# A four-layer graph network on one core: the adjacency's transpose moves from TensorE to transposing transfers on SyncE's queue

## The chip, the cores and the metric

The kernel runs on one core of a Trainium2 chip. Its time is the device time of one execution in microseconds (us), and a kernel's time is the median of its runs. The core has five engines: TensorE (PE in the profile, with its weight loads shown apart as PEld), VectorE (DVE), ScalarE (ACT), GpSimd (POOL) and SyncE (SP). SyncE only issues transfers here. ScalarE and GpSimd issue transfers as well as compute. Each engine runs its own list of instructions strictly in order; between engines there are semaphores.

## The reference, cut to what matters

There are 32 graphs ("batches") of 512 nodes with 128 features, each with a 0/1 adjacency matrix of 512 x 512 with about one entry in 32 set. Four layers follow each other, each of them layernorm, relu, a graph layer and a residual sum:

```
h = relu(layernorm(x)); x = x + L0(h, adj)   # p = h(W1-W2), q = h W2;
                                             # max over neighbours j of relu(p_i + q_j + b)
h = relu(layernorm(x)); x = x + L1(h, adj)   # 4 sublayers: adj and adj^T, l2-normed, aggregate h;
                                             # tanh([src, self, dst] @ wu + bu)
h = relu(layernorm(x)); x = x + L2(h, adj)   # rows of adj divided by their sum, times h W, plus bias
h = relu(layernorm(x)); x = x + L3(h, adj)   # 4 GRU steps on adj^T-aggregated messages
```

So each batch needs the adjacency as it lies in memory (`an`), and its transpose (`at`), and the row sums and column sums of it.

## The kernel before, in words

One batch passes through four functions: `prepare` (layer 0 up to the lists of neighbours), `gathers` (the maximum over neighbours), `layer1` (the four sublayers) and `layer23` (layers 2 and 3). They write no instructions at once. Each call is noted with the buffers it reads and writes, and the scheduler `Flow` issues all noted calls of all 32 batches in one order. That order is written out by hand, so to speak: a long table of encoded due times (`FRONT`, `MIDDLE`, `BACK`) gives every noted call a due time, and on each engine the calls go out sorted by it. About four batches are in work at once, at different stages. All calls go out from one line of `Flow.step`, L1038, so nearly all rows of the profile carry that line and one goes by the names of the tiles instead. When the scheduler expects TensorE to wait more than a microsecond, it puts in idle matmuls, `spin` (L1064), whose results nobody reads; they keep TensorE's granted clock up.

Within `prepare`, for batch b:

- ScalarE's queue has loaded `af`, the adjacency in f32, 128 partitions x 4 x 512. A check on VectorE (`junk`) finds whether each entry is 0 or 1.
- ScalarE converts `af` to bf16 in four pieces, `ab`, and sums the rows on the way (`deg`).
- TensorE transposes the sixteen 128 x 128 blocks of `ab` into PSUM (`pat`, against the bf16 identity `identb`), and ScalarE copies them out to `at` in four pieces, summing the columns on the way (L1498 to L1509).
- TensorE counts neighbours by a matmul on `at` (`pc`), ScalarE writes the counts as `cc`, and sixteen small transfers per batch on SyncE's queue spread `cc` to `ccd`. VectorE and ScalarE compare `ccd` with 1 to 4, giving the one-hot matrices `oh`.
- `pkey`, `top`, `at8` and `idx` pick up to seven more neighbours per node, and the table of q goes to memory (`qtab<-qn`, SyncE's queue).

`gathers` takes those seven by indirect transfers on GpSimd's queue (`G<-qtab,idx`), and the first four neighbours of each half tile by matmuls (`pa<-oh,qhl`, 32 per batch), whose results VectorE folds into `acc` by maximum. Then `acc` is transposed back (`px`) and folded into `gm`, and `x1` is the input of `layer1`, which begins with the aggregations `pg` and ends with the products `pu`. `layer23` ends with the sums `xo`, which are stored.

Buffers come in rings: the n-th user of a tag waits until the user `bufs` places before has been read for the last time. `junk` and `ab` share the tag `ab`, which has one buffer, so `ab` of a batch waits for its `junk`, and `junk` of the next batch waits for the last transpose of this one.

The weights are prepared by TensorE, ScalarE and SyncE in the first tens of microseconds, mixed with the first batches (`FastWeights.first`, `rest`, `last`).

Of the kernel before, what the change touches and what calls it, by code (L numbers as in the profile page):

```python
# [13 lines left out]
F32 = mybir.dt.float32  # L14
# [11 lines left out]
P = 128  # L26
# [3 lines left out]
KSLOT = 4  # L30
# [3 lines left out]
NLEFT = 7  # L34
# [3 lines left out]
PERIOD = 81.6923  # L38
# [3 lines left out]
    346.63,  # L42
    (
        "!!!!nz!)U!6%!6:!,G!;8!7/!8i!;1!M*!U=!<I!jA!}3!t<!x.!xW#,y#/W#<|#?x#@z#a4#eA#r##rd#tZ#r_#"
        "sP#sV#s}#{?#oz#q{#ro#sJ$#A#qu#r{$$3$%#$*@#ru#s##~M$$8$+Q$%T#|l$)/$+;$$T$%)$(N$&S$,b$)]$/"
        "x$2$$6n$)}$*|$,?$.=$+_$,|$*h$,0$-]$7{$.z$1H$,{$-I$9y$0h$9<$0+$-L$5M$8[$61$_!$7>$B}$C5$Gb"
        "$Gu$Ja$Ju$P@#Ap$.6$/F$2K$2^$4#$;E$.=$.D$/M$/T$1D$2m$2e$2v$3M$4:$5I$7%$:u$:{$;%$@k$A>$B+$"
        "CR$JN$D>$ML$UQ%.F$H:$E4$Md$O<$FV$Q^$I]$Qw$LA$Vm$Pa$Y;$T>$_N$Uk$bM$WI$dg$Yt$d{$`^$is$c6$k"
        "J$eB$ra$hH$q/$pB$xL$qt$z`$s=${U$u}$~-$y6%%*${<%(;$|_%(y$~f%-0%%c%7]%(t%4q%*:%6X%/^%8R$4h"
        "$7O$7{$8h$=s$8$$>R$@^$?k$DH$9)$C~$E4$F;$Gn$:&$GL$Jd$H`$LM$C]$Jm$Mr$K($P4$G0$M5$P|$R^$S.$"  # L50
        "R0$U2$W$$Ua$Wn$TX$WD$YO$X/$Z;$U:$X^$[($Y/$^1$V/$^i$cr$`X$gv$XY$hh$i6$h~$k_$g9$pw$r#$q2$u"
        "h$j+$tW$vS$vX$w?$ji$w+$yB$xr${j$u*$z-$|U$|}$}L$xa$~9%#K$~P%/N%1~%2-%2U%2l%9O%:A%?q%>1%?R"
        "%?3%3k%@G$tA$t~$z:%._%]=%[m%H%%E%%Gv%D[%H.%I@%J/%D{%I2%LU%PP%JO%Re%So%SE%Ry%TL%U&%Yc%d,%"
        "[C%`s%b:%bi%db%^q%_[%_s%`-%`~%a:%ai%b#%eC%_-%`D%`[%aQ%bE%fi%g;%h<%l0%kC%lU%mU%nP%o_%p[%p"
        "g%pr%q=%q[%r[%s+%sq%tC%tr%uZ%v-%wE%x^%y`%tZ%u-%vD%v[%vs%w.%wt%x/%xk%y/%yF%zm%|)%}7%~8%~C"
        "%~p%~{&!>&!}&#V&$@&%A&(%&)~&*h&+:&+Q&,m&#n&$)&$W&%*&&k&(T&(l&*9&,0&$o&%X&)&&+}&-1&.,&/%&"
        "05&1*&15&1K&1b&2#&3x&4$&:m&;(&;n&<?&=W&=o&@+&D$&:T&;?&;V&<V&=)&>*&?o&C&&F#&<n&GG&Il&K.&L"
        "(&M!&Mz&QQ&S|&Vy&X+&Yi&Yt&Z!&Z9&[D&`t&]9&a,&b(&a@&]X&cb&ci&d&&d?&c|&eY&en&gl&h9&hb&k0&k~"
        "&iA&pY&pr&q-&qC&qZ&rD&rs&w1&yp&|>&|S&|j&}:(#6&}d($1(#Q(%%(&6(%c(%w(&/(&z(&J(&Q(*[(*t(*S("
        ",$(,8(-/(-W(,b(.2(/.(.o(/,(/>(/I(/h(0_(1Y(2T(3&(3>(3U(4((4?(4V(4n(5<(6;(7J(7I(8h(9Y(5@(8"  # L60
        "E(8L(9S(:@(:q(;Q(<>(=3(=>(=I(=T(=s(?2(=`(?-(@((@V(@n(A)(A@(AW(B*(BA(Bl(D%(E8(E4(FF(GF(Bo"
        "(G](E}(IJ(J7(H-(K((Kq(M`(Mk(Mv(O7(OU(P8(N#(OB(Q7(Qg(R8(RO(Sz(T4(Tc(U5(Ua(V_(Y/(Wm(Z=([/("
        "WY(ZA(Xh([O(]<(]0(^-(_!(`3(`T(``(`k(a-(al(`v(ap(bk(c&(c>(cU(cm(d&(dU(eV(f%(g#(gz(h2(i<(j"
        ".(f)(i1(h{(jB(k/(l.(lk(ma(nd(nz(o.(o9(q,(oX(pn(os(qR"
# [4 lines left out]
        0.80,  # L69
        (  # L70
            "!!!!+,!*0!*t!+L!2~!(^!3@"
# [3 lines left out]
        3.00,  # L75
        (
            "!!!!!A!/a!),!,j!3T!([!1Z!.7!/4!-:!01!1.!3(!2+!.d!2W!*J!,=!7L!:1!;n!!>!:[!:{!:f!;)!:Q!=7!"
            ":q!<6!#>!%n!7f!:?!:r!;?!-g!;+!;P!<&!=&!0^!<<!<r!=H!=r!>&!>&!>=!Bn!?5!BY!Cj!)X!;-!?g!A*!A"
            "]!Fh!<w!As!BI!B|!CI!>e!CB!Ca!D7!Db!DM!DN!Dd!I.!FV!H9!I5!Ap!B@!H}!Hr!Id!JE!Jg!Lj!Bm!J|!J["
            "!LN!M[!M0!N8!DZ!ME!MP!NS!O5!Ox!PJ!OK!OK!Ob!Vv!Pg!V;!V[!Eh!I@!P`!Pv!Pk!RT!SA!TK!Tb!Vj!K?!"  # L80
            "T*!T@!T5!U5!U}!VB!Vt!WZ!Mp!V7!VX!Vd!W4!W}!Y9!Y#!ZV!XB!XB!Xj!YK!Y7!Y7!YV"
# [3 lines left out]
        3.74,  # L85
        (
            "!&6!#m!Y2!`N!bw!b2!`r!cm!!!!a$!a0!c%!dh!*,!am!b&!ax!dA!fA!gN!cE!iu!jD!j#!li!bF!j/!j9!jO!"
            "jo!kZ!m3!k?!rA!s2!sx!u?!jo!rL!rc!rx!sf!tb!v?!uq!}/!}f!}:!~g!sF!}P!}Z!}E!~@#!,##$!%Z##@#$"
            "|"
# [5 lines left out]
            "!!!!!M!!O!)5!)^!)I!)q!*K!*D!*)!*R!*m!+)!*f!,6!-@!,I!-i!,s!.!!0^!1M!2>!32!.!!.9!.O!.e!/3!"  # L95
            "3#!3C!3f!48!4V!1W!2u!38!4-!5C!1c!3Z!4N!4Y!60!1n!3O!4C!4f!7h!4q!1y!6!!6a!5l!6;!7U!7w!;O!8"
            "F!<l!?/!:S!6g!76!8U!9s!7u!96!7!!<4!<s!CY!>#!>a!79!>+!Ed!@N!FD!?n!8c!>g!B<!A[!GQ!By!91!9E"
            "!;7!;J!;_!;s!<*!8}!8z!9$!9,!93!9M!:9!9:!9@!9G!9N!;#!;m!9U!9~!:)!:;!=W!@X!=]!=d!=k!=r!DC!"
            "Gr!I`!P6!Iu!>n!G<!L7!Mx!JG!Ss!V[!Q.!RP!U9!W~!ay!YD!Zg!^R!]0!i(!a>!d&!ba!_x!oE!eI!g#!j&!m"
            "b!ul!r&!o(!pJ!sL!{z!tq!vb!x(!yJ#%?!>M!@5!Am!B<!E?!?w!Et!FN!HM!I!!@M!BB!I=!J!!Ir!Jt!Cb!IC"  # L100
            "!Jm!Kv!KR!M}!LV!MR!Nj!Mk!OU!M8!P<!Ph!PS!R*!J|!LJ!RW!S&!SK!TX!Mf!OO!Sc!UD!U~!VM!QH!V9!W9!"
            "WA!X$!Sw!WY!YG!YT!Z3!Qc!VM!Ym!]<!Z&!^(!X%![o!^=!`(!^Z!`p!^e!_a!bY!_w!cE!_F!`A!d2!a!!dz!^"
            "G!a:!be!ef!co!fR!bV!cr!eu!g>!gz!ne!oq!p.!p9!pD#&,#(N#+0#*/#*n#*N!$Z#+c!L<!K[!Ly!N|!S_!T/"
            "!S,#-^#-r#-7#.*#.P#.W#-V#.I#.q#2Z#.j#3|#5*#5S#4]#44#6-#6u!fL#5i#66#6A#6{#:L#7*#8L#8X#8e#"
            "9.#9G#9`#9y#:<#7E#8r#8~#9:#9S#9l#:)#:5#;S#:B#:N#:Z#:g#:t#;##;0#;<#>]#;I#;U#;b#;n#;{#<+#<"
            "7#<D#>~#<P#=,#<]#=9#?B#?n#@P#@=#@i#AY#A8#AC#B9#BD#B##Be#C!#CL#B[#CD#CQ#Cj#D&#D3#De#G<#Gi"
            "#Bh#C^#Cv#D?#DK#DX#Dq#E.#Ed#C!#D}#E:#EF#ES#El#Ex#F)#H9#E`#F5#FA#FM#FZ#Fg#Fs#G!#GF#G0#G`#"
            "Gl#H<#H{#IJ#J.#I}#JM#K0#K*#K<#Kl#Kw#K[#LN#L9#Mf#LF#M:#MG#NQ#Nk#R1#R=#RJ#Rj#LS#M.#MS#M`#M"
            "l#NE#N^#Nw#P4#La#O&#O3#OL#OX#Or#P.#PG#SD#O@#Oe#O~#P;#PS#P`#Pm#R##RE#Py#S%#Q)#S3#QT#U)#RV"
            "#UT#S_#V##T.#TY#U=#V^#W4#Wt#Wn#X##XZ#Xf#XB#Xs#Y)#YQ#Xz#Y_#Yl#Z?#Zd#[-#[]#[v#_r#YR#Yx#Z(#"  # L110
            "Zp#Z}#[P#[j#]=#bV#_;#_N#_Z#_h#_y#`0#`=#`I#by#`U#`b#`o#`{#a+#a7#aD#aP#cR#a]#es#aj#f;#b9#h"
            ")#be#hT#c4#i##c`#ih#d/#j7#da#jc#eG#g!#gb#k2#kv#lX#lh#n,#n6#nA#vE#wo#w4#wZ#x9#x2#wS#y@#xX"
            "#yR#{?#yY#|L#~)#~R#}3#}[$!,$&N$#u$)n$**$*A$*W$+F$+v$,1$1;$3z$5-$5Z$5q$6+$7V$6i$9|$9+$8t$"
            "9h$:E$:|$:u$;F$:n$;?$;a$>D$;X$?`$?t$@j$A7$@A$An$B[$B:$BE$BP$Cs$DI$E@$F;$G5$Ge$G|$H7$Hf$H"
            "}$I7$IN$Iz$Jq$L$$L!$M3$NU$If$M7$M.$NE$O2$P`$P!$Q}$Rr$R}$S,$S7$SU$T9$SB$U9$W/$W^$Wu$X0$XG"
            "$X_$Y1$YH$Ys$[-$]($]U$^6$_-$Y`$^:$^B$`w$b-$`:$cw$dd$eg$er$e}$g%$gE$h($f,$g1$iU$in$j)$j@$"
            "jW$k@$kW$l6$la$mu$o*$o&$p8$q6$le$p#$q?$r2$rz$s&$sx$tm$ub$ul$uw$v%$vE$w($v1$w7$x2$xI$xa$x"
            "x$y3$yJ$z4$zy${H$|F$~S$}f%!b%#_${K%!N%!V%#]%$I%$B%%:%&%%(,%(<%(R%)$%*~%*I%*d%*/%+H"
# [3 lines left out]
        5.36,  # L122
        (
            "!)C!/!!1K!0]!0H!04!23!2,!1D!2$!2E!2^!2M!3k!5I!4|!4S!4*!<G!@#!A;!BL!C=!9x!:&!:2!:=!N@!DZ!"
            "D`!Df!Dl!O?!BC!BI!CF!D7!ZZ!T8!Ub!V(!Wv!`#!U]!U~!V-!Wp!`l!WD!Vu!bz!de!af!b5!cb!c?!d~!f-!h"
            "$!hx!ja!ba!cF!dg!fe!d*!eG!c4!cx!f(!k1!h%!kn!cK!dM!lN!j#!r+!gE!cc!kn!m/!sH!tU!rh!a_!c&!ga"
            "!lM!lb!n*!q@!FJ!cy!d#!d+!d2!lX!qf!d9!d@!dG!dN!k$!kn!ho!jT!jb!kN!nC!o/!jZ!ji!j{!k%!s1!sz!"
            "uE!wZ!uZ!t@!w=!w[#)m#(G#+3#,U!v-#39!zc#0S!}$#3p!~I#9F#3x#<&#5>#>m#6a#@N#:!#B1#<_#Dy#?I#G"
            "o#A*#I5#Bj#Jt#Et#N/#HK#PV#In#R,#KP#S^#No#W.#Q3#Y=#Re#[`#T:#^=#Wg#`r#[$#d^#_E#gO#`h#i:!mM"
            "!nH!nz!ng!rP!ov!q]!te!rF!ue!m_!oO!tU!wb!tn!xM!pl!rD!v`!zM!w2!{9!y.!z*!|^!~%!~h!yl!~=#!S!"  # L130
            "~`##H!tz!yb#!7#$5##N#$}!{E!~`##f#%i#$C#&U#)w#*s#+H#+4#,4#*X#+c#,|#,5#-i#!|#)A#,d#/+#-6#/"
            "s#+O#,k#0s#1I#1K#25#.I#1c#5r#8d#:C#0h#8|#;/#97#<;#1b#2}#<M#=&#<e#?$#4=#93#<|#?n#BG#D<#FF"
            "#G$#G0#G;#iY#jv#mQ#m2#l_#l?!!!#nO!wn!y/!xN!w1#ml#n<#_!#pD#p1#oy#pr#pd#q=#pk#q5#r,#rW#r$#"
            "tv#v##u.#uV#vM#w&#wo#rZ#vc#vn#vy#w0#w]#wx#yK#yz#zL#z{#{d#{{#|6#}M#xJ#{6#{M#|M#|e#||#}7#}"
            "f#~4#}N#}}#~x$!r$$$$$v$%$$%0$%:$%Y$&<$&J$(7$(N$(f$)8$)f$*g$,!$,Y$&y$(}$)O$)}$*8$*O$*~$+P"
            "$-:$,Q$,i$-{$/1$0?$1?$1J$1U$1a$2!$2p$3!$4}$5O$69$7:$7h$8!$8Q$:Q$3:$3k$58$5g$5~$6P$6h$7P$"
# [8 lines left out]
        ),  # L145
    ),
    (
        22.66,
        (
            "!!!!2O!+u!,-!-z!/-!/H!/A!/O!/V!5t!7Z!/i!8h!FS!;q!97!=C!Q=!Sx!UL!V<!XB!b(!b3!bC!bN!c+!be!"  # L150
            "bq!bv!b|!c]!b>!bY!b`!bk!dL!c$!c1!c<!d+!e9!c+!c6!c|!d%!f%!e>!do!i;!}&!g@!ej!hu!|L#/r#0U#2"
# [2179 lines left out]
```

## Time and profile before

| what | value |
|---|---|
| median of 3 runs | 2818.99 us (2816.03 to 2822.98) |
| the profiled execution | 2812.02 us |
| its span, first to last instruction | 2810.3 us |
| mean granted clock of TensorE | 0.993 |
| TensorE busy | 2730.7 us (97%), 11169 matmul rows |
| VectorE busy | 2450.0 us (87%) |
| GpSimd, ScalarE busy | 1640.5 us (58%), 1284.4 us (46%) |

A table by stage is read so: each row is a stretch of the span, and for each engine it gives the busy microseconds and, in brackets, the number of instructions. A group gives the line, the engine, the operation, the names written and read, the shape, how often it came, then the busy time and the mean duration of one, then the idle time of that engine right before it. TensorE's matmuls overlap, so the duration of one (from its start to its modelled end) is longer than the time until the next one starts; the room that a matmul takes is the distance between starts. SPq and ACTq are the issues of transfers on SyncE's and ScalarE's queues.

### The profile page before, as it was taken

To read this page: it belongs to the slowest core of one execution; us is meant where nothing else is said; L and a number is where in the kernel's file an instruction comes from. 1 tells how busy PE (TensorE), PEld (TensorE's weight loads), DVE (VectorE), ACT (ScalarE), POOL (GpSimd) and SP (SyncE) were. 2 spreads that over 40 slices of the span, in tenths; PEclk is the share of its full clock that TensorE was granted. 3 is DMA by queue.
4 is the path that set the end of the run, shared out by engine and by line. 5 is a ranking of instruction groups with operands and counts; after the bars stand their busy time and mean duration, and the time that the engine had idled before them with its cause. 6 is when DMAs were issued, how large, how long until landed. Compare 5 with 4: busy or idle time off the path is not lost.

```text
span 2810.3 us, 36776 instructions
## 1 busy us (share of the span) xinstructions
PE 2730.7 (97%) x11169; PEld 1743.4 (62%) x11169; DVE 2450.0 (87%) x5739; ACT 1284.4 (46%) x2623; POOL 1640.5 (58%) x1892
## 2 busy tenths in 40 slices
PE   7799999999999999999999999999999999999997
PEld 4466666666666666666666666666665656666675
DVE  7788999999999999999999999999998988988533
ACT  7644444444444444444444444445444344434333
POOL 5676665566656556665656665665666666665311
PEclk9999999999999999999999999999999999999999
DMA  7743334343344443434444333344433433333100
GB/s 170 131 77 74 68 75 88 83 81 79 70 76 89 89 84 78 81 70 77 89 81 92 73 79 70 83 90 80 92 68 73 91 85 80 62 61 57 36 4 9
DMA packets 188177, 217.59 MB, mean 77 GB/s; under 512 B 28826, under 2 KB 136516, under 8 KB 187972
## 3 DMA queue, kind: packets, MB, share of 16 engines
q0 software_dynamic: 47104, 92.34, 24.4%
q1 hardware_dynamic: 73540, 64.62, 7.8%
q10 hardware_dynamic: 67328, 58.20, 6.6%
q8 instruction: 91, 1.49, 0.2%
q14 instruction: 114, 0.93, 0.1%
HBM read 164.32 MB, written 17.17 MB: 65 GB/s over the span
## 4 chain that ended last, share of the span: by engine, by line
PE 82%; DVE 7%; POOL 2%; issue 2%; ACT 2%; DMA 1%; SPq 0%; DVEq 0%; ACTq 0%; POOLq 0%
PE pg L1038 25%; PE pu L1038 19%; PE pk L1038 14%; PE pa L1038 7%; PE phn L1038 4%; PE pxn L1038 3%; PE ph L1038 2%; PE pq L1038 2%; PE pf L1038 1%; PE pt L1038 1%; DVE nn L1038 1%; DVE acc L1038 1%; PE po L1038 1%; PE px L1038 1%; PE pkey L1038 1%
## 5 line engine op out<-in xcount | busy, mean ns | idle before, releaser
L1038 POOL DMA_INDIRECT G<-qtab,idx x744 | 794.5, 1068 | 464.7 <-DVE gm L1038 277.1
L1038 DVE TENSOR_TENSOR acc<-acc,pa 128x512 f32<-128x512 f32 x992 | 676.3, 682 | 57.8 <-PE pa L1038 32.0
L1038 PE MATMUL pa<-oh,qhl 128*128 128x512 f32 x1024 | 490.8, 504 | 5.9 <-DVE oh L1038 2.5
L1038 PE MATMUL pg<-an,hi 128*128 128x512 f32 (+1 forms) x1072 | 471.4, 445 | 1.8 <-ACT hi L1038 1.4
L1038 PE MATMUL pu<-ag,w 128*128 128x512 f32 (+1 forms) x952 | 445.8, 574 | 0.1
L1038 PE MATMUL pg<-an,lo 128*128 128x512 f32 (+1 forms) x1072 | 401.9, 389 | 1.4 <-DVE lo L1038 1.4
L1038 DVE TENSOR_SCALAR oh<-ccd 128x1024 fp32r<-128x1024 bf16 x492 | 338.6, 699 | 15.0 <-DMA ccd<-cc 7.5
L1038 ACT ACTIVATE xn<-x,shift,rstd 128x128 f32<-128x128 f32 x512 | 222.0, 486 | 173.0 <-POOL shift L1038 138.6
L1038 PEld LDWEIGHTS pa<-oh,qhl 128*128 128x128 f32 x1024 | 190.9, 190 | 133.9 <-issue 57.4
L1038 PE MATMUL pg<-at,hi 128*128 128x512 f32 (+1 forms) x672 | 273.5, 422 | 0.4 <-DVE lo L1038 0.3
L1038 PEld LDWEIGHTS pg<-an,hi 128*128 128x128 f32 x1072 | 202.0, 188 | 97.0 <-issue 42.1
L1038 PE MATMUL pk<-mT,g_ih 128*128 128x512 f32 (+1 forms) x528 | 257.4, 584 | 1.2 <-ACT mT L1038 1.2
L1038 ACT ACTIVATE gate<-pk,bsum 128x512 f32<-128x512 f32 (+1 forms) x264 | 176.5, 673 | 175.8 <-PE pk L1038 138.5
L1038 PE MATMUL pk<-h,g_hh 128*128 128x512 f32 (+1 forms) x528 | 253.0, 586 | 0.4 <-ACT h L1038 0.2
L1038 PE MATMUL pg<-at,lo 128*128 128x512 f32 (+1 forms) x672 | 250.0, 387 | 1.1 <-POOL lo L1038 0.7
L1038 PEld LDWEIGHTS pu<-ag,w 128*128 128x128 f32 x952 | 168.8, 190 | 113.1 <-issue 94.5
L1038 PEld LDWEIGHTS pg<-an,lo 128*128 128x128 f32 x1072 | 201.7, 188 | 57.1 <-issue 10.3
L1038 ACT COPY mT<-pg 128x512 f32<-128x512 f32 (+1 forms) x164 | 94.2, 574 | 273.3 <-PE pg L1038 237.5
L1038 DVE TENSOR_TENSOR gm<-gm,G 128x128 f32<-128x128 f32 x744 | 212.8, 292 | 2.0 <-DMA G<-qtab,idx 1.9
L1038 POOL TENSOR_TENSOR rstd<-rstd,mhalf 128x4 f32<-128x4 f32 x128 | 143.7, 1126 | 106.8 <-DVE rstd L1038 62.1
L1038 DVE TENSOR_TENSOR ag<-pg,rbc 128x512 f32<-128x512 f32 (+1 forms) x272 | 173.8, 650 | 22.7 <-PE pg L1038 22.4
L1038 POOL TENSOR_SCALAR zc<-gate 128x512 f32<-128x512 f32 (+1 forms) x132 | 81.0, 614 | 165.1 <-ACT gate L1038 164.5
(179 smaller groups left out, 5245.0 us busy)
## 6 DMA issues: line engine op xcount, KB each, us to landing
ccd<-cc SPq DMA_DIRECT2D x512, 64.0 KB
an<-in_adj_dram POOLq DMA_DIRECT2D x128, 256.0 KB, 4.2
af<-in_adj_dram ACTq DMA_DIRECT2D x31, 1024.0 KB
x<-in_x_dram ACTq DMA_DIRECT2D x64, 256.0 KB
rbc<-scal SPq DMA_DIRECT2D x32, 512.0 KB
G<-qtab,idx POOLq DMA_INDIRECT x744, 3.7
qtab<-qn SPq DMA_DIRECT2D x32, 256.0 KB
out_dram<-xo ACTq DMA_DIRECT2D x32, 256.0 KB
```

The lines of the kernel that those rows point to most:

```text
L1038: op.fn(*(real(v) for v in op.args), **{k: real(v) for k, v in op.kw.items()})
```

## The change

Six things change. The sixteen transposes per batch on TensorE, and their PSUM banks `pat`, are gone. `ab` becomes four tiles of 128 x 512 in a ring of two buffers. Each is transposed by one transposing transfer, issued by SyncE from SBUF to SBUF, into a new tile `abt` (128 x 4 x 512 bf16, one buffer), and ScalarE reads `abt` in place of `pat` when it writes `at`. `junk` moves to the tag of `abt`, and for the first batch to the tag of `oh`. A one-column square root on ScalarE comes first of all, so that its function table is loaded first. The input `x` of the first two batches stays in SBUF instead of being loaded a second time; `qn` moves to the tag `xn0`. And the encoded order of all instructions is new, from a scheduler whose entries for transfers were changed as well. The new constants (`KSLOT`, `NLEFT` as tuples, `KEPT` empty) keep their values, so that what they switch does not change.

```diff
-KSLOT = 4
+KSLOT = (4, 4)
-NLEFT = 7
+NLEFT = (7, 7)
+KEPT = ()
...
     def first(self):
+        F.act.activation(self.own([P, 1], F32, "root"), self.ones[:, 0:1], AF.Sqrt)
...
     def load(b):
-        xt = F.tile(mid, [P, NT, D], F32, tag="xin", name=f"x_{b}")
+        xt = F.tile(mid, [P, NT, D], F32, tag="x1" if b < 2 else "xin", name=f"x_{b}", bufs=2 if b < 2 else 1)
...
-        junk = F.tile(big, [P, NT * N], BF16, tag="ab", name=f"junk_{b}")
+        junk = F.tile(
+            big, [P, NT * N], BF16, tag="oh" if b == 0 else "abt", name=f"junk_{b}", bufs=3 if b == 0 else 1
+        )
...
-        ab = F.tile(big, [P, NT, N], BF16, tag="ab", name=f"ab_{b}")
+        abs_ = []
         for t in range(NT):
+            ab = F.tile(big, [P, N], BF16, tag="ab", name=f"ab_{b}_{t}", bufs=2)
             F.act.activation(
-                ab[:, t, :], af[:, t, :], AF.Identity, accum_out=deg[:, 0, t : t + 1]
+                ab, af[:, t, :].bitcast(F32) if b in KEPT else af[:, t, :], AF.Identity,
+                accum_out=deg[:, 0, t : t + 1],
             )
+            abs_.append(ab)
...
-        for half in range(NT // 2):
-            pt = bank(0, [P, 2, N], BF16, f"pat_{b}_{half}")
-            for u in range(2):
-                jt = 2 * half + u
-                for it in range(NT):
-                    F.tr(
-                        pt[:, u, it * P : (it + 1) * P],
-                        ab[:, it, jt * P : (jt + 1) * P], W.identb,
-                    )
-                F.act.activation(
-                    at[:, jt, :], pt[:, u, :], AF.Identity, accum_out=deg[:, 1, jt : jt + 1]
-                )
+        abt = F.tile(big, [P, NT, N], BF16, tag="abt", name=f"abt_{b}")
+        for it in range(NT):
+            F.sync.dma_start_transpose(out=abt[:, :, it * P : (it + 1) * P], in_=abs_[it])
+        for jt in range(NT):
+            F.act.activation(
+                at[:, jt, :], abt[:, jt, :], AF.Identity, accum_out=deg[:, 1, jt : jt + 1]
+            )
...
-        x1 = F.tile(mid, [P, NT, P], F32, tag="x1", name=f"x1_{b}", bufs=2)
-        F.act.dma_start(out=x1, in_=x[b].rearrange("(t p) d -> p t d", p=P))
+        x1, an = xt, af
+        if b >= 2:
+            x1 = F.tile(mid, [P, NT, P], F32, tag="x1", name=f"x1_{b}", bufs=2)
+            F.act.dma_start(out=x1, in_=x[b].rearrange("(t p) d -> p t d", p=P))
```

## The prediction

> **What bounds the kernel now.** I read the page's busy table first, then the windows by stage, then TensorE's waits in the steady part, then the rows that the change removes, then the start.
>
> The busy table:
>
> ```profile
> PE 2730.7 (97%) x11169; PEld 1743.4 (62%) x11169; DVE 2450.0 (87%) x5739; ACT 1284.4 (46%) x2623; POOL 1640.5 (58%) x1892
> ```
>
> 97% is an average, so the windows come next: the start, the steady part, the run-out and the last batches. Columns are the stretch, its length, busy us of PE, PEld, DVE, ACT and POOL, granted clock, DMA share, GB/s.
>
> ```profile
> 0.00:326.80 326.80, 283.92 (x1291) 184.33 (x1292) 270.52 (x658) 178.39 (x366) 203.15 (x258) 0.96 0.55 107
> 326.80:2091.00 1764.20, 1761.43 (x7081) 1120.42 (x7081) 1629.34 (x3801) 817.93 (x1669) 1080.26 (x1243) 1.00 0.40 80
> 2091.00:2634.00 543.00, 530.27 (x2080) 329.51 (x2078) 478.18 (x1093) 228.02 (x468) 332.39 (x359) 1.00 0.38 73
> 2634.00:2810.30 176.30, 155.12 (x722) 109.09 (x720) 71.99 (x191) 60.05 (x123) 24.66 (x34) 0.97 0.03 9
> ```
>
> In the steady 1764 us TensorE is idle for 2.8 us. VectorE is at 92%, ScalarE at 46%, the DMA engines at 40%. The view of TensorE's own waits from 500 to 1980 us has two rows, 1.5 us in all:
>
> ```profile
> PE ph L1038 <- DVE h L1038: 1.3, 2, 1.0
> PE pk L1038 <- ACT mT L1038: 0.2, 1, 0.2
> ```
>
> So in this part nothing but TensorE's own work sets the pace: 18 batches in these 1480 us, 82.2 us each. Work taken from TensorE there is worth its whole time, until VectorE's 75.6 us per batch (its busy time in the window from 1500 to 1581.7) becomes the bound, 6.6 us lower.
>
> **Part 1: the transposes leave TensorE.** The built program has 512 matmuls `pat` and 512 weight loads less, and 128 transposing transfers on SyncE's queue more, so the change does what it says. The view of tile `pat` gives the duration, the timeline of TensorE from 1509 us the room:
>
> ```profile
> L1038 PE MATMUL pat<-identb,ab x512: 216/219/314, 14.2 to 2533.9; 128*128 128x128 bf16 x171
> ```
> ```profile
> 1510.39 0.39 PE L1038 MATMUL pat<-identb,ab 128*128 128x128 bf16 x4
> 1510.62 0.50 PE L1038 MATMUL pf<-ident,f 128*128 128x128 f32 x3
> 1510.95 0.33 PE L1038 MATMUL pat<-identb,ab 128*128 128x128 bf16 x3
> 1511.12 0.28 PE L1038 MATMUL ph<-ident,h 128*128 128x128 f32 x1
> ```
>
> One lasts 219 ns but four make room for the next kind after 1510.62 - 1510.39 = 0.23 us, three after 0.17: 57 ns each. A batch loses 16 x 57 ns = 0.91 us, all batches 29.2 us. For batches 0 to 3 the transposes stand before TensorE is saturated (about 240 us), so on the path lie 28 x 0.91 = 25.5 us.
>
> The Trainium skill speaks against this: "VectorE: DVE Perf Modes", section "The three transpose paths", gives 390 ns for a bf16 128x128 on TensorE and 1309 ns through the DMA crossbar, and advises TensorE where PSUM will do. By its 390 ns the removal would be worth 16 x 0.39 = 6.2 us a batch, some 175 us in 28; the row above decides against that, because transposes overlap. By its 1309 ns a transfer of four blocks would take an estimated 5.2 us, which no row here shows.
>
> **Part 2: what hides the new transfers.** Each moves 128 KB, four per batch. The trace of before has no transposing transfer, so bounds are from neighbours, here the queues and three issue rows (KB each, us to landing):
>
> ```profile
> q0 software_dynamic: 47104, 92.34, 24.4%
> q1 hardware_dynamic: 73540, 64.62, 7.8%
> an<-in_adj_dram POOLq DMA_DIRECT2D x128, 256.0 KB, 4.2
> G<-qtab,idx POOLq DMA_INDIRECT x744, 3.7
> two<-qtab,idx POOLq DMA_INDIRECT x24, 7.5
> ```
>
> q1, which carries SyncE's kinds of transfers by its bytes, moved 64.62 MB in 7.8% of 2810 us, 219 us: 128 KB take 0.4 us. At q0's rate (92.34 MB in 686 us) they take 1.0 us. So the moving is 0.4 to 1.0 us, the landing 3.7 to 7.5 us. I take 1.0 and 4.2 us, the slower queue and the nearest size above. That is 4 us of DMA engines per batch where 60% of 82 us is free.
>
> The landing is hidden. In the new order `at` of a batch is read some 40 ScalarE instructions after its last `ab`, beginning just after the store of the batch three before. In the trace of before the like stretch, from the first `acc` copy (1540.8) to the next `xo` (1595.5), lasts 55 us; the landing would have to grow tenfold. ScalarE's own work stays: `at` from PSUM took 598 ns each, `ab` from SBUF 620, so 4 x 22 ns more, on an engine busy at 46%.
>
> Not so far from the path is SyncE's queue. In the new order the first transfer of batch b+1 stands ahead of the first `ccd<-cc` of batch b, the second and third stand among its other `ccd` pieces, and the first must also wait for `junk` of b+1 on VectorE, which now shares a buffer with `abt`. Behind it queue 16 `ccd`, `qtab`, `rbc`, `row`; VectorE's `oh` and then TensorE's `pa` wait for `ccd`. The queue in before:
>
> ```profile
> 1529.52 3.67 SPq L1038 DMA_DIRECT2D ccd<-cc  x6
> 1533.23 0.56 SPq L1038 DMA_DIRECT2D scal<-sct  x1
> 1533.89 5.27 SPq L1038 DMA_DIRECT2D ccd<-cc  x4
> ```
>
> A piece takes 0.61 us to issue, four 2.4 us, and at a gather's 3.3 us for 64 KB (`gm`, the nearest row of that size) they land at about 1535.3. The first `oh` starts at 1537.78: 2.5 us of slack. An issue of 0.4 to 1.3 us (an ordinary row, or two of them) fits in; I count nothing.
>
> **Part 3: the start.** The windows from 0 to the first `acc`, then to the moments at which batches 0, 1 and 2 have `x1`:
>
> ```profile
> 0.00:31.40 31.40, 21.91 (x108) 12.35 (x108) 17.07 (x59) 18.04 (x51) 10.61 (x44) 0.95 0.62 181
> 31.40:107.00 75.60, 54.61 (x265) 34.17 (x264) 59.65 (x128) 56.01 (x113) 48.67 (x56) 0.89 0.90 162
> 107.00:172.00 65.00, 56.49 (x339) 45.33 (x339) 55.23 (x135) 33.43 (x62) 39.20 (x46) 1.00 0.50 93
> 172.00:237.00 65.00, 62.46 (x237) 37.81 (x238) 57.30 (x142) 31.35 (x63) 47.12 (x50) 0.95 0.41 72
> ```
>
> Here VectorE leads, 189 us busy of 237, and latencies show.
> - Later: batch 0's chain. In before `ab` began at 13.4 us and the last `at` at 21.7. Now four conversions (0.8 us each) go through two buffers, so the third waits for the first transfer: two round trips of about 4 us, then four `at` of 0.8 us. Sixteen small weight loads (0.25 to 0.45 us each in the first microseconds) stand between the first two transfers on SyncE. Together 8 to 13 us; I take 10.
> - Later: the new order lets TensorE begin batch 0's `pg` only after batch 1's `px`. By counting instructions times the room of each, 74 us of TensorE's work then lie between the `px` of batches 1 and 2, in place of 61, while VectorE has 66. That is up to 8 us.
> - Earlier: most of layer 1's weights are prepared while batch 0 waits, so that VectorE's idle time of 16 us in the second window and 10 in the third can shrink, by some 8. The order has 3.5 us less VectorE work ahead of batch 2's `px` (197 us against 201). The second function table load (1.28 us at 15.34) leaves the chain. Two loads of `x` (256 KB each) fall away in the window with DMA at 0.90, price 0 to 1 us.
> - `junk` of batch 0 in another buffer: it ended at 10.6 us and `ab` began at 13.4, so nothing.
>
> Bounds: if the weights hide all of the later start, -3.5 - 1.3 = -5; if nothing is hidden, 13 + 8 - 5 = +16. I take 10 + 8 - 8 - 3.5 - 1.3, about +5. A sign of a longer start is that the order has 161 idle matmuls there, 94 before; how long the gaps are it does not tell.
>
> **Part 4: the end.** The latest 30 us of TensorE's work, from the last but one batch's result on, are the same in both orders, and the idle matmuls there are 48 in place of 54. I count nothing.
>
> **The sum.** -25.5 + 5 = -20.5 us on the profiled execution's 2812.0 (span 2810.3), so 2791.5. The median of the three runs shown is 2819.0, 7.0 us above the profiled one; carried over, **2798.5 us**.
>
> **Rivals.**
> - *The start eats the gain.* It loses the whole 16 us or some more, say 18: 2819 - 25.5 + 18 = 2811.5, no change. For it: 67 more idle matmuls, and TensorE's late `pg`. Against it: VectorE leads there and has less to do.
> - *SyncE's queue holds `ccd` up (slower).* One mechanism: a transposing transfer keeps SyncE or its rings longer than 2.5 us, so that `oh` comes late and TensorE, which has no slack, waits at `pa` in each of 28 batches. It decides from 2.5 + 20.5/28 = 3.2 us per transfer. At 4.2 us it costs 28 x 1.7 = 48: 2798.5 + 48 = 2846; at 7.5 us 28 x 5 = 140. For it: the place in the queue and that no such transfer is in the trace. Against it: by both queues' rates the moving is 1 us at most.
> - *The start gets shorter:* -25.5 - 5 = -30.5, 2788.
>
> **The numbers.** The main case 0.66, the shorter start 0.08, the start that eats the gain 0.12, SyncE's queue 0.14. From no change this measurement can tell about 0.3%, 8.5 us (2810.5 to 2827.5). Faster 0.74, within 0.12, slower 0.14. The main case alone, with the start's bounds, is 2788 to 2810. The range goes from 2784 (shorter start and 4 us of scatter) to 2824, which takes in the case of no change and leaves out most of SyncE's.
>
> **What would show it.** Right: in the steady part the batches follow at about 81.3 us, TensorE's idle there stays at a few us, `pat` is gone, `at<-abt` waits for no DMA, the third batch's `x1` comes at about 242 us. Wrong: rows "DVE oh <- DMA ccd" or "PE pa <- DVE oh" in each batch; the transposing rows on SPq above 2.5 us; or an idle TensorE in the first 240 us beyond 16 us more than before.

## The result, and the profile after

The changed kernel takes 2829.07 us (median of 6 runs, 2827.85 to 2831.26) against 2818.18 us for the kernel before on the same chip (6 runs): a ratio of 1.0038, 95% interval 1.0025 to 1.0051. It is 0.4% slower, where 0.7% faster was forecast. The profiled execution took 2828.67 us (span 2827.0) against 2812.02 before, 16.7 us more, where the medians are 10.9 apart: before's profiled execution lies 6.2 us under the median of its runs here, after's at its median. Some 6 us of what follows on the two traces are thus scatter between executions.

The same views as before the prediction, now of the kernel after. The busy table and the windows (stretch, length, busy us of PE, PEld, DVE, ACT and POOL, granted clock, DMA share, GB/s):

```profile
PE 2723.7 (96%) x10703; PEld 1719.5 (61%) x10718; DVE 2432.8 (86%) x5739; ACT 1268.1 (45%) x2623; POOL 1730.0 (61%) x1892
```
```profile
0.00:326.80 326.80, 282.16 (x1241) 181.05 (x1251) 263.98 (x633) 177.34 (x364) 196.53 (x246) 0.96 0.62 115
326.80:2091.00 1764.20, 1746.48 (x6684) 1090.83 (x6683) 1606.95 (x3783) 791.44 (x1654) 1158.49 (x1241) 1.00 0.44 86
2091.00:2634.00 543.00, 523.75 (x2015) 328.77 (x2014) 482.41 (x1114) 232.96 (x472) 343.83 (x366) 1.00 0.41 78
```

In the steady stretch TensorE is now idle for 1764.2 - 1746.5 = 17.7 us, where it was 2.8. The view of TensorE's waits from 500 to 1980 us names what it waits for:

```profile
PE ph L1051 <- ACT f L1051: 5.0, 16, 0.3
PE ph L1051 <- DVE h L1051: 3.3, 2, 2.8
PE pf L1051 <- ACT f L1051: 0.7, 2, 0.4
```

A transpose `ph` waits for ScalarE's `f` in 16 of 18 batches; before, it did not once. The new transfers do not occur in this view. Their own view, tile `abt`, shows what they cost and who waited for them:

```profile
L1051 SPq DMA_TRANSPOSE abt<-ab x128: 1189/1216/4964, 13.6 to 2479.5; - x128
L1051 ACT ACTIVATE at<-abt x128: 612/618/643, 33.1 to 2487.4; 128x512 fp32r<-128x512 bf16 x128
...
who waited for it (us, times):
  POOL dm L1051: 22.6, 4
  ACT ab L1051: 8.2, 2
```

SyncE issues one in 1.2 us in the median, inside the 0.4 to 1.3 us of the prediction. VectorE's `oh` waits for a `ccd` transfer once in the whole run, for 3.8 us. Both waits of `ab` for a transfer lie in the first 101 us. So in the steady part nothing was lost at the new transfers themselves; the time went elsewhere.

Two measures tell where. The first is the period, the median distance between the last `xo` rows of successive batches, batches 5 to 20. The forecast was 81.3 us; it is 82.27, where before had 82.20. The second is the time of the last `xo` of a batch against the kernel before: 11.5 us later at batch 0, 16.0 at batch 3, 16.2 at batch 9, 21.5 at batch 11, 20.8 at batch 21, 16.7 at the end. So the start lost 16 us, the steady part gained nothing and lost 5 us once, and batches 22 to 24 gained some 4.

### The profile page after: what moved, and what is told of

The parts are those of the page before. It is cut to its first block, busy times and chain, and to the rows that moved or that the text cites. A ratio compares the mean times of both kernels' runs of the same rounds, so it can differ in the third digit from the quotient of the medians.

```text
span 2827.0 us, 36274 instructions
## 1 busy us (share of the span) xinstructions
PE 2723.7 (96%) x10703; PEld 1719.5 (61%) x10718; DVE 2432.8 (86%) x5739; ACT 1268.1 (45%) x2623; POOL 1730.0 (61%) x1892
## 3 DMA queue, kind: packets, MB, share of 16 engines
q1 hardware_dynamic: 143172, 81.41, 11.7%
## 4 chain that ended last, share of the span: by engine, by line
PE 79%; DVE 10%; POOL 4%; issue 4%; ACT 3%; DMA 1%; SPq 0%; DVEq 0%; ACTq 0%; POOLq 0%
PE pg L1051 24%; PE pu L1051 18%; PE pk L1051 13%; PE pa L1051 6%; PE phn L1051 3%; PE pxn L1051 3%; PE ph L1051 2%; DVE nn L1051 2%; DVE acc L1051 2%; PE pq L1051 2%; PE pf L1051 1%; POOL G L1051 1%; PE pt L1051 1%; PE po L1051 1%; PE pkey L1051 1%
## 5 line engine op out<-in xcount | busy, mean ns | idle before, releaser
L1051 POOL DMA_INDIRECT G<-qtab,idx x744 | 829.3, 1115 | 380.6 <-DVE gm L1051 172.7
L1051 PE MATMUL pa<-oh,qhl 128*128 128x512 f32 x1024 | 482.3, 497 | 15.9 <-issue 6.3
L1051 PE MATMUL pg<-an,hi 128*128 128x512 f32 (+1 forms) x1072 | 464.1, 439 | 4.4 <-ACT hi L1051 3.7
L1051 PE MATMUL pg<-an,lo 128*128 128x512 f32 (+1 forms) x1072 | 413.4, 392 | 0.0
L1051 DVE TENSOR_SCALAR oh<-ccd 128x1024 fp32r<-128x1024 bf16 x492 | 344.8, 703 | 7.1 <-DMA ccd<-cc 3.8
L1051 PE MATMUL pg<-at,lo 128*128 128x512 f32 (+1 forms) x672 | 265.3, 398 | 1.5 <-POOL lo L1051 1.3
L1051 PE MATMUL pk<-h,g_hh 128*128 128x512 f32 (+1 forms) x528 | 245.1, 586 | 0.6 <-ACT h L1051 0.5
L1051 POOL TENSOR_TENSOR rstd<-rstd,mhalf 128x4 f32<-128x4 f32 x128 | 162.4, 1269 | 114.7 <-DVE rstd L1051 89.0
L1051 POOL TENSOR_TENSOR lo<-xn,hi 128x512 fp32r<-128x512 f32 x96 | 123.2, 1283 | 139.4 <-ACT hi L1051 138.6
```

Of the source, the lines that this page charges most:

```text
L1051: op.fn(*(real(v) for v in op.args), **{k: real(v) for k, v in op.kw.items()})
```

## The experiments

Theory A: the new order is at fault; it brings waits of its own that take the freed time, in the start and in each batch. Theory B: the transposing transfers slow something, GpSimd above all, whose semaphores last 208 ns in place of 59 and whose gathers `G` 1135 ns in place of 1058. Theory C: TensorE's time was never worth its whole, since other engines' chains lie right behind it. All kernels were timed against the kernel before on their own chip.

| kernel | ratio to before, 95% interval | median, us | period, us |
|---|---|---|---|
| before | 1 | 2812.7 to 2818.2 by chip | 82.20 |
| after | 1.0038 (1.0025 to 1.0051) | 2829.07 | 82.27 |
| after, again | 1.0041 (1.0029 to 1.0053) | 2831.74 | 82.28 |
| e1: old order, transfers | 0.9940 (0.9926 to 0.9953) | 2796.39 | 81.38 |
| e2: transposes twice | 1.0074 (1.0061 to 1.0088) | 2834.04 | 83.11 |
| e4: after, plain copies | 1.0066 (1.0052 to 1.0080) | 2832.60 | 82.28 |
| e5: after, more TensorE work | 1.0138 (1.0123 to 1.0154) | 2851.78 | 83.33 |
| e7: e1 with more batches | 0.9935 (0.9923 to 0.9947) | 2800.48 | 81.40 |
| e8: after, batch 0 on TensorE | 1.0046 (1.0033 to 1.0059) | 2831.51 | 82.28 |
| e9: e1, table and `x` | 0.9937 (0.9924 to 0.9950) | 2800.70 | 81.40 |
| e12: work in the wait | 1.0063 (1.0047 to 1.0079) | 2830.00 | 82.26 |
| e14: work elsewhere | 1.0077 (1.0061 to 1.0093) | 2835.37 | 82.49 |

Four kernels with the order of after have periods of 82.27 to 82.28: the period is good to about 0.02 us, far better than the total time.

**e1_old_order_dma: the transfers in the old order.** The kernel before, with its table of due times, and only the transposes of batches 5 to 25 moved.

```diff
+        if b in MOVED:                       # range(5, 26)
+            abt = F.tile(big, [P, NT, N], BF16, tag="abt", name=f"abt_{b}")
+            for it in range(NT):
+                F.sync.dma_start_transpose(out=abt[:, :, it * P : (it + 1) * P], in_=abs_[it])
...
+    junk = max(due[s - 10], at + 0.9)
+    ab[2], ab[3] = max(ab[2], ab[0] + 7.0), max(ab[3], ab[1] + 7.0)
+    return (due[: s - 10] + [junk] + ab + due[s - 5 : s] + [t + 0.9 for t in ab] + ...
```

> Kernel before, its start and its order, with the transposes of batches 5 to 25 alone moved to SyncE's transposing transfers (each due 0.9 us after its ab; the four at follow each other at the place of the first; junk writes to the buffer of abt; some small rings are shortened for room). TensorE loses 21 x 0.91 = 19.1 us of work. Theory A (the new order is at fault, not the transfers): about 2799 us (2795 to 2806), batches follow at 81.3 us. Theory B (the transfers themselves slow other engines, GpSimd above all): no gain, 2817 or more, period 82.2 or more, and GpSimd's semaphores and gathers longer as in after. Theory C (other engines' chains lie right behind TensorE, so that its time is worth only a part): 2808 to 2818, period between 81.7 and 82.2, and TensorE idle some tenths of a us in each batch.

Measured: 2796.39 us, 17.4 below before, period 81.38. TensorE's busy time in the steady stretch of e1:

```profile
326.80:2091.00 1764.20, 1758.23 (x6815) 1120.60 (x6815) 1640.51 (x3841) 824.72 (x1677) 1095.33 (x1252) 1.00 0.47 87
```

and its waits from 500 to 1980 us:

```profile
PE ph L1055 <- DVE h L1055: 0.8, 1, 0.8
PE pf L1055 <- ACT f L1055: 0.3, 1, 0.3
PE pk L1055 <- ACT mT L1055: 0.2, 1, 0.2
```

TensorE stays busy, idle 6.0 us in 1764, and the waits at `f` in every batch are not there. This is theory A: the same transfers bring 0.82 us per batch of the 0.91 forecast, if the order stays. It is also faster than both kernels of the case. Order is not all that sets e1 apart from after: after also has other buffers for `qn` and `hi2`, and no run took these apart from the order. The waits that after shows are for `f`, `mT` and `h`, whose tags are the same in both.

**e2_pat_twice: the price of a transpose.**

```diff
                 for it in range(NT):
-                    F.tr(pt[:, u, it * P : (it + 1) * P], ab[:, it, jt * P : (jt + 1) * P], W.identb)
+                    for again in range(1 if b < 4 else 2):
+                        F.tr(pt[:, u, it * P : (it + 1) * P], ab[:, it, jt * P : (jt + 1) * P], W.identb)
```

> Kernel before with each of the transposes of the adjacency done twice in batches 4 to 31 (448 more, same place, same data). If a transpose makes 57 ns of room and TensorE sets the pace (theories A, B, C alike for more work): 448 x 57 ns = 25.5 us more, about 2844 us (2840 to 2848). If one costs what it lasts (219 ns) it is 98 us more, about 2916. If TensorE does not set the pace in before: under 2825.

Measured: 20.3 us more, somewhat under the 25.5 expected. In the steady part the price is exact: the period rises from 82.20 to 83.11, by 0.91 us for 16 transposes: 57 ns each, as read from the distances between starts. Neither the 219 ns that one lasts nor the 390 ns of the Trainium skill ("VectorE: DVE Perf Modes", "The three transpose paths") is what it costs here.

**e4_plain_copy: are the transposing transfers to blame?**

```diff
-            F.sync.dma_start_transpose(out=abt[:, :, it * P : (it + 1) * P], in_=abs_[it])
+            F.sync.dma_start(
+                out=abt[:, :, it * P : (it + 1) * P], in_=abs_[it].rearrange("p (t c) -> p t c", c=P)
+            )
```

> Kernel after, with each transposing transfer replaced by a plain transfer of the same bytes between the same buffers at the same place (leaves out the transposition, so that at holds the matrix untransposed, and the count that would start the slow path is set to 0). Theory A (order) and C: as after, 2829 us (2824 to 2833), period 82.2. Theory B (transposing transfers slow others): about 2805 to 2815, period 81.3 to 81.7, GpSimd's semaphores and gathers as short as in before (59 ns, 1058 ns).

Measured: ratio 1.0066, period 82.28, so no gain at all from taking the transposition away. GpSimd's groups from 500 to 1980 us, first in e4, then in after, are alike:

```profile
L1051 POOL DMA_INDIRECT G<-qtab,idx x432 | 490.0, 1134 | 204.3 <-DVE gm L1051 70.9 <-issue 50.0 <-DVE xo L1051 36.8
```
```profile
L1051 POOL DMA_INDIRECT G<-qtab,idx x432 | 490.1, 1135 | 204.6 <-DVE gm L1051 71.7 <-issue 56.0 <-DVE xo L1051 37.0
```

while e1, with transposing transfers, has 1055 ns and gains. The longer rows do not come from the transposition, and theory B falls. Nor does the order alone make them: e5, below, has the order of after and 1062 ns.

**e5_after_more_pe: has TensorE room in after?**

```diff
+        if 4 <= b < 25:
+            for half in range(2):
+                more = bank(0, [P, 2, N], BF16, f"more_{b}_{half}")
+                for k in range(8):
+                    F.tr(more[:, k // 4, (k % 4) * P : (k % 4 + 1) * P], W.identb, W.identb)
```

> Kernel after with 16 more bf16 transposes of 128 x 128 on TensorE in each of batches 4 to 24 (of the identity, results read by nobody), just ahead of at: 21 x 0.91 = 19.1 us of work put back. If TensorE sets the pace in after: about 2848 us. Theories A and C (TensorE waits for other engines in each batch, so has room): a part of it, 2829 to 2840.

Measured: 1.0138 against 1.0038 to 1.0041 for after, some 27 us more, and the period 1.06 us longer. Those were other chips; against e4, which has the same order and ran on the same chip, it is 19.2 us more, for the 19.1 us of work put in. This went against what theories A and C had been read to say: although TensorE waits in each batch, its work still counts in full. The waits are links of TensorE's own chain, not room beside it. With e1 this settles theory C too: in either order TensorE's work is worth its time.

**e12_work_in_wait and e14_work_elsewhere: the wait itself.** The timeline of after around one of the waits (start, us, engine, line, operation, in brackets the idle time before it):

```profile
1364.72 1.02 PE L1051 MATMUL pu<-ag,w 128*128 128x512 f32 x2
1365.18 1.03 PE L1051 MATMUL pa<-oh,qhl 128*128 128x512 f32 x2
1365.78 0.69 ACT L1051 ACTIVATE f<-pu,bu 128x512 f32<-128x512 f32 x1 [1.66 <-PE pu L1051]
1366.52 0.30 PE L1051 MATMUL ph<-ident,h 128*128 128x128 f32 x1 [0.31 <-ACT f L1051]
```

`pu` ends, ScalarE makes `f` of it, and the order gives TensorE only two `pa` to do meanwhile. `ph` of another batch comes next and starts 0.05 us after `f` has ended; the profile names `f` as what released it. It reads nothing that `f` writes; a PSUM bank that `f` has to read first would make it wait so, which is not shown. By the distances between starts 0.42 us are lost there. The two kernels put four more transposes into this place, and into a place 2 us later.

```diff
                 if s == 0 and t == NT - 1 and int(name.split("_")[1]) in TWICE:      # range(8, 26)
+                    for k in range(4):
+                        F.tr(pt[:, t, :], src[:, t, :], W.ident)
...
+                due = due[:26] + [due[26] - EARLIER] * 4 + due[26:]                   # 2.06 in e12, 0.001 in e14
```

> Kernel after, with one f32 transpose (the fourth pt of layer 0) done five times instead of once in batches 8 to 25, the four extra ones (4 x 0.11 = 0.44 us) right ahead of the ph of the batch four before, where the trace of after shows TensorE waiting 0.42 us for ScalarE's f (16 of 18 batches). If that wait of the new order is real and stands in TensorE's own chain, the work fits into it: 0 to 2 us above after (1.004 to 1.005 of before). If TensorE's waits are not where the time goes (its work counts wherever it stands, as in e5): 18 x 0.44 = 7.9 us more, 1.0068 of before.

> The same four extra transposes in batches 8 to 25 of kernel after, but right ahead of the fourth pt itself, some 2 us of TensorE's work later, where the trace shows no wait. Both theories: 18 x 0.44 = 7.9 us more than after, 1.0068 of before; it is the price against which e12 is held.

Measured: the totals differ by 5.4 us with overlapping intervals (both 1 to 2 thousandths above what was expected), so the periods decide: 82.26 with the work in the wait, the same as after, and 82.49 with it elsewhere. There its rows take 0.44 us (the five `pt` from 1454.38 to the next start at 1454.85, where one had 0.03), of which half is made up by short waits that after has behind this place and e14 has not. The row `ph` after the added work in e12 has no idle time before it:

```profile
1448.20 0.60 PE L1054 MATMUL pt<-ident,xn 128*128 128x128 f32 x4
1448.69 0.30 PE L1054 MATMUL ph<-ident,h 128*128 128x128 f32 x1
```

So the wait is real, it stands in the chain, and its length is what the rows show.

**e8_after_pat0: the start.** Batch 0's transposes alone back on TensorE, its conversions one after the other.

```diff
+            if b == 0:
+                ab = whole[:, t, :]
...
+                at = [15.0, 15.8, 16.6, 17.4]
+                due = due[:20] + [11.1, 11.9, 12.7, 13.4] + due[24:29] + [
+                    v for t in at for v in [t - 0.9] * 4 + [t]
+                ] + due[37:]
```

> Kernel after, with batch 0's transposes alone put back on TensorE and their conversions one after the other, so that batch 0's at is there at about 22 us in place of 36; all else and its order as in after. If the first batch's two round trips of transfers (10 us in the prediction) make the start late: the first acc comes some 10 us earlier and the time falls by up to 10 us (0.9965 of after). If the new order makes it late (it has the weights' work ahead of batch 0's on each engine): less than 2 us, and the first acc stays near 47 us.

Measured: as after (1.0046 against 1.0041 on the same chip). The last `at` of batch 0 starts at 19.5 us in place of 37.1, and still the first `acc` comes at 52.1 us, 48.7 in after on that chip. The round trips of the first batch, 10 us in the prediction, are not what makes the start late.

**e11_after_again: after, once more.**

> Kernel after, unchanged, on the same chip as the others of this call, to compare e8 with: 1.0038 of before (1.0025 to 1.0051).

Measured: 1.0041, as the first time.

**e7_old_order_more and e9_old_order_root_x: what else in the old order?** e7 moves the transposes of batches 5 to 31, e9 adds the square root's table and the kept `x` to e1.

```diff
-MOVED = range(5, 26)
+MOVED = range(5, 32)                                                                   # e7
...
+        F.act.activation(self.own([P, 1], F32, "root"), self.ones[:, 0:1], AF.Sqrt)    # e9
...
+        x1 = xt
+        if b >= 2:
```

> As e1_old_order_dma, but with the transposes of batches 5 to 31 moved (27 in place of 21), the conversions of a batch further apart (10 us in place of 7 between the first and the third). Theory A (in the old order a freed us of TensorE is worth what e1 showed, 17.4 us for 21 batches, 0.83 each): the last batch has nothing behind it and batches 26 to 30 have other, tighter orders, so up to 5 x 0.83 = 4 us less than e1's 2796.4 at its before of 2813.8, that is 0.9925 of before. If the conversions' waits for the two buffers stall ScalarE in the last batches: as e1 or up to 8 us more.

> As e1_old_order_dma, with two more parts of the change in the old order: the square root's table first on ScalarE, and x of batches 0 and 1 kept in place of a second load. By the prediction -1.3 us for the table and 0 to -1 for the loads: 1.3 to 2.3 us below e1. If the table load does not lie on the path or what is saved is waited for elsewhere: as e1.

Measured: 0.9935 and 0.9937 against e1's 0.9940, all within each other's intervals. The six more batches bring nothing that can be told, and neither do the table and the loads, priced at 1.3 to 2.3 us. What is left to make the start of after some 16 us later is its order, with the transfers of batches 1 to 4 and the new buffers, which no run took apart from it.

## Why the prediction was wrong

**Part 1, the price: right.** 57 ns a transpose is what e2 shows, and e1 gives back 0.82 of 0.91 us per batch.

**Part 1, the sum: the step that failed.** "Work taken from TensorE there is worth its whole time" was read from a trace in the old order, and the 25.5 us were then booked for a kernel with a new one. The new order has waits that no row of before could show. In a batch of after, 0.42 us are lost at `ph <- f`, 0.28 at `pk <- mT` (a row with 12 to 26 ns of idle time, but started 0.28 us late), and 0.25 in a stretch of four `pu` and three `ph` between two `pa`, 0.95 us together; in e1 the first two are seen once each at most. The 0.91 us that the transposes left were gone again, and the period stayed at 82.27. The prediction's own test, that "TensorE's idle there stays at a few us", is where it shows: 17.7 us. The gain was in the plan: the constant `PERIOD`, the distance of the batches in the table of due times, is 81.69 us in before and 80.81 in after. The chip ran the old order 0.51 us over its plan and the new one 1.46.

**The loss of 5 us once.** At batch 10 the new order lets GpSimd's `zc` stand behind three gathers and a `lo`. VectorE waits 3.44 us for it, then TensorE:

```profile
1114.19 0.62 POOL L1051 TENSOR_SCALAR zc<-gate 128x512 f32<-128x512 f32 x1
1114.84 0.69 DVE L1051 TENSOR_TENSOR gate<-h,gate 128x512 f32<-128x512 f32 x1 [3.44 <-POOL zc L1051]
1116.25 0.68 DVE L1051 TENSOR_TENSOR h<-gate,nn 128x512 f32<-128x512 f32 x1
1117.08 0.45 PE L1051 MATMUL ph<-ident,h 128*128 128x128 f32 x1 [2.83 <-DVE h L1051]
```

It comes at the same place in each of the seven traces with this order (2.4 us in e12, 2.8 in the others), and in none with the old one, where batch 17 loses 1.2 to 1.3 us once (before, e1). Why in this batch and not in its neighbours, whose order is the same, stays open.

**Part 2: right for the steady part.** There is no wait for the transfers there, and no `oh` behind `ccd`. In the start the landing kept to neither of its bounds, 3.7 and 7.5 us. Batch 0's second transfer was issued at 21.81 us and had released its buffer at 24.24, 2.4 us later; the plain copy in e4 took 2.3. Batch 2's second took 11.0 us, and ScalarE waited for it; the plain copy in e4 took 12.5:

```profile
89.08 4.96 SPq L1051 DMA_TRANSPOSE abt<-ab  x1
100.12 0.63 ACT L1051 ACTIVATE ab<-af 128x512 bf16<-128x512 f32 x1 [5.98 <-DMA abt<-ab]
```

By the 1309 ns per block of the Trainium skill ("VectorE: DVE Perf Modes", "The three transpose paths") four blocks would take an estimated 5.2 us; batch 0's took less than half of that.

**Part 3: the yardstick was wrong.** The third batch's `x1` came at 241.3 us, as forecast ("about 242"), and at 246.7 in the trace of after, again. But from there TensorE sets the pace, and what counts is how much of its work is still to do. Each matmul counted by the room of its kind (the median distance to the next start in the steady part of before) and the idle ones by nothing, before had 2506.1 us of work left at 240 us, 25.1 of them transposes that the change removes, so 2481.0; after has 2489.8. It is 8.8 us behind at the very moment at which `x1` says 4. At 490 us it is 15.4 behind (2255.1 against 2262.1 - 22.4). The idle matmuls hide this in the busy time, 197.8 us of 240 against 198.5: after has 152 of them in that stretch, before 94. The prediction saw the 67 more in the order and set them aside because their gaps were unknown. Its price of 10 us for batch 0's round trips fell with e8, and the 1.3 us for the table could not be seen in e9; so its items added up to the right `x1` without being right one by one, which was luck.

The start scatters: the last `xo` of batch 3 ends between 526.2 and 533.7 us in four traces with the old order (before, e1, e7, e9), between 542.1 and 546.1 in five with the new one (after twice, e4, e12, e14). The new order's start is later in each, by 8 to 20 us. A place where it may lose shows in the chain of work that ended last: from 75 to 99 us it runs through two transfers of SyncE's queue, while the DMA engines are full (the window below, DMA share 1.04). The weight load among them, issued at 88.18 us, was issued at 57.32 in before. First the chain of after, then its window, then the issue in before:

```profile
75.13 11.83 DMA ccd<-cc
88.18 11.17 DMA w<-in_L_gnn_weight_dram
```
```profile
89.00:101.00 12.00, 7.31 (x18) 3.22 (x18) 8.45 (x23) 5.99 (x11) 1.54 (x2) 0.64 1.04 135
```
```profile
57.32 0.40 SPq L1038 DMA_DIRECT2D w<-in_L_gnn_weight_dram  x1
```

The prediction had no term for a wait for this load. No experiment moved this load, so its share of the 16 us is not shown.

**Part 4: right.** From the last `xo` of batch 24 to the end nothing changes (16.9 us later, then 16.7). The 4 us that after gains lie before that, between batches 21 and 24, which Part 4 did not price.

**The rivals.** SyncE's queue, the slower one, did not come: 1.2 us is under the 2.5 us from which it decides. "The start eats the gain" had the start right (18 us assumed, some 16 measured), but gave no change because it too kept the 25.5 us. What happened, a new order with waits in every batch, was not among the rivals, though the order was known to be new.

What stays open: which part of the new order makes the start late. Giving batch 0 or the weights their old place inside the new order was not tried.

## What to carry to other kernels

A trace in which one engine is saturated prices work taken from it only as long as the order of that engine stays; when a change brings a new order with it, price the change and the order apart, and look in the new order for places where little of the saturated engine's work stands between a result and its next use. A wait in the saturated engine's chain costs as much as work there, and work put into it is free: the period of the steady part shows both to 0.02 us where the total time scatters by 3. Measure a start by the work that the later bottleneck still has to do, not by a milestone on another engine's path, and count idle matmuls as nothing.

## What the runs showed of the hardware

- A transposing transfer of 128 x 512 bf16 on SyncE's queue takes 1.2 us to issue, where a plain one of the same bytes takes 0.63, and lands about as fast (2.4 against 2.3 us at batch 0, 11.0 against 12.5 at batch 2, where the DMA engines are full). With 128 of them the queue's busy share is 11.7% in after, with 128 plain copies 10.3% in e4.
- TensorE's granted clock fell after the single wait of 2.83 us in batch 10, and stayed low for several microseconds:

```profile
1117.00:1124.00 7.00, 6.92 (x23) 5.62 (x24) 5.64 (x13) 0.59 (x1) 4.31 (x6) 0.56 0.38 39
```

  Seven us at 0.56 of the clock are 3.1 us of work missed; with the wait that is 5.9, where 5.2 us were lost. In the seven traces with this order the clock went to half around this place, for at least 3.4 us, in six; in e14, after the same 2.83 us, it stayed at 1.00, and 3.0 us were lost in place of 5.2. The Trainium skill ("TensorE: Matmul & The Clock Gate", "HAM oscillation — how this bites in real kernels") sets the limit at idle gaps above some 3.4 us; here a shorter one was enough, though not each time.
- The same GpSimd instructions do not always last the same. Gathers took 1134 to 1140 ns in the mean in six traces with the order of after, with transposing or plain transfers, but 1062 in e5, which has that order too; in the old order they took 1045 to 1058. Semaphores took 208 ns in after, 158 in e1 and 59 in before. What makes the difference stays open.
